# Layer 1's expert routing taken batch by batch into the attention to the context, in a decoder kernel on one core

## The chip, the cores and the metric

The kernel runs on one core of a Trainium2 chip. The metric is device time in microseconds (us). A core has five engines, each with a queue of its own that it works through in order: PE (matrix products; PEld is its loading of weights), DVE (vector), ACT (scalar functions), POOL and SP (which here issues DMAs). They wait for one another by semaphores.

## The reference

The program is one pass of a decoder over 8 batches of 256 tokens with 256 features. Four layers each do self-attention, attention to a context (120 rows for each batch) and a feed-forward part, each followed by a layer norm of the sum with its input. The change concerns layer 1, its attention to the context and its feed-forward part, which is a mixture of 32 experts:

```
logits = x @ gate_w.T                       # 2048 tokens x 32 experts
topk_w, topk_idx = top_k(softmax(logits), 4);  topk_w /= sum(topk_w)
# sorted by expert, then by token: pos = place of the token in its expert's list
slot = minimum(pos, 256)                    # 256 rows for each expert
buf[expert, slot] = x[token]
expert_out = (silu(buf @ w_gate) * (buf @ w_up)) @ w_down
routed[token] += expert_out[expert, slot] * topk_w      # where pos < 256
out = routed + (silu(x @ shared_gate) * (x @ shared_up)) @ shared_down
```

The place of a token in an expert's list is the number of earlier choices of the same expert, so the batches are bound together by running counts. The rows that an expert takes (the "take") are the lists turned round: for each expert and place the number of the token.

## The kernel before, in words

X lies in 16 tiles of 128 tokens, two for each batch; xT is its transpose. Code is written as functions for each part of a layer. A scheduler sets the order of instructions in each engine's queue within what dependencies, buffers and the order of the code allow; a tile pool has a fixed number of buffers for each tag, and a tile waits until the buffer that it takes over has been released.

**Attention to the context, layer 1** (`l1_xattn`, L792, which calls `attention16`, L703). A loop runs over the 8 batches. An iteration for batch b has: exponentials of b's scores (`exps16`; PE scores, ACT exp L627, buffers of the tag e0, two of 8 KB for each partition); the largest scores of batch b+1 (`largest16`, DVE reductions to `low`, L572; `lower16`, L609); the output projection, residual and layer norm of batch b-1 (`project_out`, L688: z L693, statistics L176 and L177, the reciprocal root on POOL L154 and L156, X L200); the keys and values of a later attention (`context3`, L833); the transposes of batch b-1 (`turn`, L696) and then its gate (`choose`, L818). Last come the sums of batch b (`sums16`, L665, and `divided16`, L645: transposes L651, reciprocals L654, `sides` on ACT L660 and DVE L661, aT on POOL L663). After an even batch the next two batches are projected (`pair`). After the loop `for step in before: step()` runs `project_out` and `turn` of batch 7.

`choose(b)` stores the two tiles of X to DRAM (L821, from which the experts gather), makes the logits (PE; ACT copies them as lg, L827) and takes the eight largest and their indices (DVE, L830 and L831).

Behind the loop stand eight sums of absolute weights of a later layer on ACT, `size` (L863), with buffers of the tag e0 too, and additions of partial sums on POOL (L865).

**Routing and experts** (`l1_ffn`, L1328). SP loads the shared expert's weights sgu and sd. POOL sums w_sums over partitions (an all-reduce, L1342). The shared expert's first product runs over 8 pieces of 256 tokens (8 fp32 matmuls, silu on ACT and a product on DVE, L1224 and L1225, into shT). `route1` (L1227) then routes all 16 tiles at once: `oh` says for token, choice and expert whether it was chosen (L1239); counts before each tile (L1254); places by products with a triangle and with ones (`pos`, L1261 and L1262) and DVE's at_own and place (L1266 to L1274); `own`, tile number and row number of each token at its expert (DVE L1258, ACT L1257). For every tile and choice `at` says which of 256 places the token has: 48 on DVE (L1282), 16 on ACT in two steps (off L1285, at L1286). 128 matmuls sum at times own into `found` (L1288), and `take` is made of it (L1295). Slots and weights are turned by 32 small matmuls (L1320) for a later stage.

The loop over 32 experts follows: its weights `we` (SP, three buffers), two gathers of 128 rows (POOL, L991, called from `gathered_T`), transposes, two products with silu between them, and the store of y. Every fourth expert also adds two tiles of the shared expert's second product. Work for a later layer is woven in.

Of the kernel before, what the change touches and what calls it, by code (L numbers as in the profile page):

```python
# [11 lines left out]
F32 = mybir.dt.float32  # L12
# [8 lines left out]
P = 128  # L21
# [25 lines left out]
class Net:  # L47
    def __init__(self, ctx: ExitStack, tc: tile.TileContext, ins, out):
# [52 lines left out]
        self.ahead = {}  # L101

# [600 lines left out]
    def attention16(self, project, low, vps, sizes, causal, wo, bo, work, then=None, ready=None):  # L703
# [45 lines left out]
        for step in before:  # L749
            step()  # L750
# [41 lines left out]
    def l1_xattn(self, w):  # L792
        nc = self.nc
        wq, wk, wv, wo, wk3, wv3, bv, bo = w
        with ExitStack() as ctx:
# [18 lines left out]
            zero = work.tile([1, D], F32, name="zero", bufs=1)  # L814
# [32 lines left out]

            def inside(b):
                return lambda: None, lambda: context3(b), lambda: None
# [3 lines left out]
                ready=(lambda: None, lambda: None, inside),  # L853
            )
# [372 lines left out]
    def route1(self, E, K, C, pool, work, ps, keep):  # L1227

        nc = self.nc
        fi = pool.tile([P, NT, K], F32, name="fi")
        nc.vector.tensor_copy(fi, self.top1_i[:, :, :K])
        iota = pool.tile([P, C], BF16, name="iota_bf")
        for o in range(0, C, 64):
            nc.vector.tensor_scalar(iota[:, o : o + 64], self.cst("iota"), float(o), None, ALU.add)
        oh = pool.tile([P, K, NT, E], BF16, name="oh")
        for k in range(K):
            nc.vector.tensor_tensor(  # L1239
                oh[:, k],  # L1240
                self.cst("iota")[:, :E].unsqueeze(1).to_broadcast([P, NT, E]),
                fi[:, :, k : k + 1].to_broadcast([P, NT, E]),
                ALU.is_equal,
            )
        m2 = pool.tile([P, 2, NT, E], BF16, name="m2")
        m = pool.tile([P, NT, E], BF16, name="m")
        before = pool.tile([P, NT + 1, E], BF16, name="before")
        nc.vector.memset(before[:, 0, :], 0.0)
        own = pool.tile([P, K, 2, NT, E], BF16, name="own")
        with nc.allow_low_precision(reason="whole numbers of at most 256"):  # L1250
            nc.vector.tensor_tensor(m2, oh[:, :2], oh[:, 2:], ALU.add)
            nc.vector.tensor_tensor(m, m2[:, 0], m2[:, 1], ALU.add)
            for i in range(NT):
                nc.vector.tensor_tensor(before[:, i + 1, :], before[:, i, :], m[:, i, :], ALU.add)  # L1254

        for i in range(NT):
            nc.scalar.mul(own[:, :, 1, i, :], oh[:, :, i, :], float(i))  # L1257
        nc.vector.tensor_scalar(own[:, :, 0], oh, self.cst("token")[:, 0:1], None, ALU.mult)  # L1258
        pos = ps.tile([P, NT, E], F32, name="pos")
        for i in range(NT):  # L1260
            nc.tensor.matmul(pos[:, i, :], lhsT=self.earlier, rhs=m[:, i, :], start=True, stop=False)  # L1261
            nc.tensor.matmul(pos[:, i, :], lhsT=self.ones_bf, rhs=before[:, i, :], start=False, stop=True)  # L1262
        pos_bf = pool.tile([P, NT, E], BF16, name="pos_bf")
        nc.scalar.copy(pos_bf, pos)
        at_own = pool.tile([P, K, NT, E], BF16, name="at_own")
        nc.vector.tensor_tensor(at_own, oh, pos_bf.unsqueeze(1).to_broadcast([P, K, NT, E]), ALU.mult)  # L1266
        part = at_own.rearrange("p k t e -> p (k t) e")
        for n in (E // 2, E // 4):
            half = pool.tile([P, K * NT, n], BF16, name=f"half{n}")
            with nc.allow_low_precision(reason="one of them is not zero"):  # L1270
                nc.vector.tensor_tensor(half, part[:, :, :n], part[:, :, n:], ALU.add)
            part = half
# [55 lines left out]
    def l1_ffn(self, w):  # L1328
# [3 lines left out]
        with (  # L1332
# [30 lines left out]
            with (  # L1363
# [31 lines left out]
                for _ in ready:  # L1395
                    pass
# [1152 lines left out]
```

## Time and profile before

Three runs took 2208.16, 2210.34 and 2219.71 us. One more execution was profiled.

| | |
|---|---|
| median of the three runs | 2210.34 us |
| the profiled execution | 2212.67 us |
| its span, first to last instruction | 2210.9 us |
| mean granted clock of PE | 0.929 |
| busy: PE, DVE, ACT, POOL | 1898.2, 1555.0, 903.1, 681.7 us |
| store of X of batch 0, and of batch 7 | at 722.27 and 848.65 us |
| last logits copied (lg ends) | at 852.43 us |
| first gather of an expert's rows | at 890.70 us |

Times in a timeline count from the start of the span. A line of a timeline has the start, the length, engine, line, operation, output and inputs with their shapes, a count where equal ones are put together, and in brackets how long the engine was idle before, with what ended the idle time. "issue" there means that the profile shows nothing that was waited for.

### The profile page before, as it was taken

What the parts mean: (1) busy time and instruction counts of PE and PEld (TensorE: products, weight loads), DVE (VectorE), ACT (ScalarE), POOL (GpSimd) and SP (SyncE); (2) the same over time, 40 slices, a digit from 0 to 9 for tenths busy, and PEclk for the clock granted to TensorE, in tenths of its full rate; (3) what the DMA queues carried; (4) which work ended last, traced back from release to release, by engine and by line L of the source; (5) the groups of instructions that cost most, each with busy time, mean ns of one, the idle gap of its engine ahead of it and who ended that gap; (6) DMA issues with size and microseconds to landing.
All of it is one profiled execution on the core that took longest, in us unless ns stands there. A gap on an engine that the chain in (4) does not pass through costs nothing. (4 is left out here: it accounts for less than half of the span.)

```text
span 2210.9 us, 37517 instructions
## 1 busy us (share of the span) xinstructions
PE 1898.2 (86%) x13553; PEld 1395.7 (63%) x13564; DVE 1555.0 (70%) x5150; ACT 903.1 (41%) x2002; POOL 681.7 (31%) x739
## 2 busy tenths in 40 slices
PE   7997699799999997897888876767899999998886
PEld 5765588655556665674455543456777777876775
DVE  6766443356666776773677678879999999976675
ACT  1333333233343336221334432534465545656663
POOL 1012244311111110544442100336544444430232
PEclk9999699999999997898899988888999999999998
DMA  4000354300002111684110010123322233320000
GB/s 139 2 2 11 117 179 148 121 26 2 1 1 86 43 43 65 179 241 140 46 40 22 1 72 1 55 77 110 87 80 76 68 89 87 86 89 14 6 15 21
DMA packets 71540, 148.55 MB, mean 67 GB/s; under 512 B 16984, under 2 KB 39912, under 8 KB 68272
## 3 DMA queue, kind: packets, MB, share of 16 engines
q0 software_dynamic: 32640, 79.46, 12.4%
q1 hardware_dynamic: 34074, 59.22, 8.2%
q10 hardware_dynamic: 4630, 7.36, 1.0%
q8 instruction: 111, 1.82, 0.3%
q14 instruction: 85, 0.70, 0.1%
HBM read 170.42 MB, written 23.24 MB: 88 GB/s over the span
## 5 line engine op out<-in xcount | busy, mean ns | idle before, releaser
L991 POOL DMA_INDIRECT rows<-in_l2f_table_dram,index x240 | 253.6, 1057 | 280.1 <-PE po L1784 59.8
L145 PE MATMUL pp<-xT,w 128*128 128x256 f32 (+1 forms) x672 | 175.3, 403 | 12.2 <-ACT sim L1490 4.6
L663 POOL TENSOR_TENSOR aT<-sides,inv 128x256 f32<-128x256 f32 x64 | 47.0, 737 | 367.8 <-DVE sides L661 271.9
L145 PEld LDWEIGHTS pp<-xT,w 128*128 128x128 f32 x672 | 127.1, 196 | 37.3 <-ACT sim L1490 5.7
L187 ACT COPY xT<-pt 128x512 f32<-128x512 f32 x88 | 51.3, 585 | 200.8 <-PE pt L186 200.6
L186 PE MATMUL pt<-ident,X 128*128 128x128 f32 x352 | 70.3, 314 | 67.0 <-DVE X L200 41.6
L1784 PE MATMUL po<-rows,diag 128*128 128x256 f32 x384 | 108.7, 403 | 12.5 <-ACT diag L1783 12.0
L627 ACT ACTIVATE e<-sc 128x512 f32<-128x512 f32 (+1 forms) x146 | 77.4, 602 | 102.2 <-PE sc L555 69.8
L991 POOL DMA_INDIRECT xe<-xd,take x83 | 83.7, 1008 | 110.9 <-DVE take L1295 36.7
L555 PE MATMUL sc<-kv,qv 32*128 32x128 f32 (+2 forms) x1520 | 109.8, 327 | 6.6 <-DVE sides L661 3.7
L555 PE MATMUL sc<-qv,kv 32*128 32x128 f32 (+2 forms) x1352 | 107.1, 352 | 2.4 <-DVE sides L661 1.4
L154 POOL TENSOR_SCALAR rs_v<-ln_mv 128x2 f32<-128x2 f32 (+1 forms) x67 | 18.8, 282 | 289.2 <-DVE ln_mv L177 238.5
L186 PEld LDWEIGHTS pt<-ident,X 128*128 128x128 f32 x352 | 45.4, 155 | 99.1 <-issue 42.7
L145 PE MATMUL sc<-xT,w 128*128 128x512 f32 x220 | 104.4, 624 | 2.9 <-DMA w<-in_l0a_wq_dram 2.2
L555 PEld LDWEIGHTS sc<-kv,qv 32*128 32x128 f32 x1520 | 86.5, 198 | 30.9 <-issue 18.6
L200 DVE TENSOR_SCALAR X<-z,ln_mv,rs_y 128x256 f32<-128x256 f32 x144 | 55.1, 425 | 59.4 <-POOL rs_y L156 59.3
L1149 ACT ACTIVATE hT<-ph,we_in 128x128 f32<-128x128 f32 x152 | 55.8, 367 | 96.6 <-PE ph L145 81.8
L1702 DVE SCALAR_TENSOR_TENSOR junk<-rows,X 128x256 f32<-128x256 f32 x224 | 94.2, 421 | 1.3 <-DVE dots L1773 0.2
L555 PEld LDWEIGHTS sc<-qv,kv 32*128 32x128 f32 (+1 forms) x1352 | 76.3, 196 | 26.5 <-issue 16.3
L145 PE MATMUL ph<-xeT,we_in 128*128 128x128 f32 x608 | 89.8, 292 | 1.3
L145 PEld LDWEIGHTS ph<-xeT,we_in 128*128 128x128 f32 x608 | 79.7, 198 | 12.3 <-ACT hT L1149 9.8
L1784 PEld LDWEIGHTS po<-rows,diag 128*128 128x128 f32 x384 | 68.0, 193 | 28.2 <-ACT diag L1783 16.7
(580 smaller groups left out, 5172.6 us busy)
## 6 DMA issues: line engine op xcount, KB each, us to landing
we<-in_l1f_experts_dram SPq DMA_DIRECT2D x32, 384.0 KB, 4.2
yd<-y SPq DMA_DIRECT2D x32, 256.0 KB, 3.9
w<-in_l2x_w_dram SPq DMA_DIRECT2D x1, 4096.0 KB
v<-v SPq DMA_DIRECT2D x16, 243.8 KB, 2.9
rows<-in_l2f_table_dram,index POOLq DMA_INDIRECT x240, 3.4
xd<-X SPq DMA_DIRECT2D x8, 257.0 KB, 2.8
xT<-in_xT_dram SPq DMA_DIRECT2D x4, 512.0 KB, 7.7
X<-in_x_dram ACTq DMA_DIRECT2D x8, 256.0 KB, 6.1
```

The lines of the kernel that those rows point to most:

```text
L145: self.nc.tensor.matmul(out, lhsT=lhsT, rhs=rhs, start=n == 0, stop=n == last and bias is None)
L154: nc.gpsimd.tensor_scalar(v, var, LN_EPS, None, ALU.add)
L186: nc.tensor.transpose(pt[:, c, j, :], self.X[:, i0 + j * step, c * P : (c + 1) * P], self.ident)
L187: nc.scalar.copy(self.xT4[:, :, i0 : i0 + step + 1 : step, :], pt)
L200: nc.vector.tensor_scalar(self.X[:, i, :], z[:, j, :], mv[:, j, 0:1], r[:, j : j + 1], ALU.subtract, ALU.mult)
L555: nc.tensor.matmul(sc[: shape[0], part], lhsT=lhsT, rhs=rhs, start=mask is None, stop=True, skip_group_check=True)
L627: lambda r, sc: nc.scalar.activation(e0[m][:n0, r], sc, AF.Exp),
L663: nc.gpsimd.tensor_tensor(out, split(both), split(inv), ALU.mult)
L991: return self.nc.gpsimd.indirect_dma_start(out=out, out_offset=None, in_=table, in_offset=bass.IndirectOffsetOnAxis(ap=index, axis=0), **( ...
L1149: nc.scalar.activation(hT[:, g + f, :], ph[:, f, :], AF.Gelu, bias=b1[:, g + f : g + f + 1])
L1702: nc.vector.scalar_tensor_tensor(junk, row, 1.0, x, ALU.mult, ALU.mult, accum_out=out)
L1784: nc.tensor.matmul(po, lhsT=diag, rhs=rows[:, k, D:], start=j == 0 and (g, k) == (0, 0), stop=j == 1 and (g, k) == (groups[-1][0], here_k ...
```

## The change

`route1` is taken apart. `begin_route1` allocates before the attention. `places1(b)` makes one-hot, counts, pos and places of one batch, `takers1(b)` its own, at and found, summed over batches into `found1`; `shared1(b)` is the shared expert's first product of one batch. The loop's iteration b runs `places1(b-2)` first and, for b of 2 to 5, `takers1(b-2)` last. After the loop, ahead of `project_out` of batch 7: places of 6, takers of 4 and 5, shared 0, 1, 2; ahead of its `turn`: takers of 6, shared 3 and 4; behind it: places and takers of 7, `end_route1` (the take, and logits less the largest), shared 5, 6, 7. The silu of `shared1` takes buffers of the tag e0. sgu and shT come from a pool that is open from ahead of the attention to the end of `l1_ffn`, and the row of zeros is the first of shT. `at_own` and pos are fp32, `off` has one buffer, `oh` four. Slots are turned after expert 2 (`slots1`), weights after the last expert (`weights1`), each with 16 of the 32 small matmuls. The `size` sums and the all-reduce are where they were in the code. The core of the diff:

```diff
@@ -746,7 +747,9 @@
-        for step in before:
+        for fill, step in zip(tail, (*before, lambda: None)):
+            if fill:
+                fill()
             step()
 
     def project16(self, dst, w, src, bias, n, kind):
@@ -811,7 +814,7 @@
                     self.values16(vp[:, n, 0, :], pv, SC, bv)
                 return qv, kv
-            zero = work.tile([1, D], F32, name="zero", bufs=1)
+            zero = self.shT[0:1, :D]
             nc.gpsimd.memset(zero, 0.0)
             nc.sync.dma_start(self.xd1[0:1, :], zero)
@@ -845,12 +848,40 @@
                 nc.vector.tensor_copy(v[:, :, :64], pv[:SC].rearrange("p (h d) -> p h d", d=64))
                 nc.sync.dma_start(self.v3[b], v.rearrange("p h d -> p (h d)"))
+            INLOOP = 4
+
             def inside(b):
-                return lambda: None, lambda: context3(b), lambda: None
+                def early():
+                    if b >= 2:
+                        self.places1(b - 2, work)
+
+                def last():
+                    if 2 <= b < 2 + INLOOP:
+                        self.takers1(b - 2, work)
+
+                return early, lambda: context3(b), last
+
+            def fill(places, takers, shared):
+                def steps():
+                    if places is not None:
+                        self.places1(places, work)
+                    for n in range(max(len(takers), len(shared))):
+                        for b in takers[n : n + 1]:
+                            self.takers1(b, work)
+                        for b in shared[n : n + 1]:
+                            self.shared1(b, work)
+
+                return steps
+
+            def finish():
+                fill(B - 1, [B - 1], [])()
+                self.end_route1(work)
+                fill(None, [], [5, 6, 7])()
             self.attention16(
                 project, low, vps, [SC], False, wo, bo, work, then=choose,
                 ready=(lambda: None, lambda: None, inside),
+                tail=(fill(B - 2, list(range(INLOOP, B - 2)), [0, 1, 2]), fill(None, [B - 2], [3, 4]), finish),
             )
             o = 0
@@ -1224,138 +1255,160 @@
-    def route1(self, E, K, C, pool, work, ps, keep):
...
+    def places1(self, b, work):
+        tiles = slice(2 * b, 2 * b + 2)
+        fi = self.fi1[:, tiles]
+        nc.vector.tensor_copy(fi, self.top1_i[:, tiles, :K])
+        oh = self.oh1[b % 4]
+        nc.vector.tensor_tensor(
+            oh,
+            self.cst("iota")[:, :E].unsqueeze(1).unsqueeze(1).to_broadcast([P, K, 2, E]),
+            fi.rearrange("p t k -> p k t").unsqueeze(3).to_broadcast([P, K, 2, E]),
+            ALU.is_equal,
+        )
+        here, following = self.counts1[b % 2], self.counts1[1 - b % 2]
+        with nc.allow_low_precision(reason="whole numbers of at most 256"):
+            nc.vector.tensor_reduce(here[:, 1:], oh.rearrange("p k t e -> p t e k"), AX.X, ALU.add)
+            if b + 1 < B:
+                nc.vector.tensor_reduce(following[:, 0, :], here.rearrange("p t e -> p e t"), AX.X, ALU.add)
+        pos = self.bank([P, 512])[:, : 2 * E].rearrange("p (t e) -> p t e", t=2)
+        for out, lhsT, rhs in (
+            (pos, self.earlier, here[:, 1:]),
+            (pos[:, 0], self.ones_bf, here[:, 0]),
+            (pos[:, 1], self.ones_bf, here[:, 0]),
+            (pos[:, 1], self.ones_bf, here[:, 1]),
+        ):
+            nc.tensor.matmul(out, lhsT=lhsT, rhs=rhs, start=lhsT is self.earlier, stop=True, skip_group_check=True)
+        at_own = work.tile([P, K, 2, E], F32, name="at_own", bufs=1)
+        nc.vector.tensor_tensor(at_own, oh, pos.unsqueeze(1).to_broadcast([P, K, 2, E]), ALU.mult)
+        nc.vector.tensor_reduce(self.place1[:, :, tiles], at_own, AX.X, ALU.add)
+    def takers1(self, b, work):
+        oh = self.oh1[b % 4]
+        own = work.tile([P, K, 2, 2, E], BF16, name="own", bufs=1)
+        nc.vector.tensor_scalar(own[:, :, 0], oh, self.cst("token")[:, 0:1], None, ALU.mult)
+        for j in range(2):
+            nc.scalar.mul(own[:, :, 1, j, :], oh[:, :, j, :], float(2 * b + j))
+        found = self.bank([P, 512])[:, : 4 * E].rearrange("p (b a e) -> p b a e", b=2, a=2)
+        for j in range(2):
+            for k in range(K):
+                at = work.tile([P, C], BF16, name="at", bufs=4)
+                where = self.place1[:, k, 2 * b + j : 2 * b + j + 1]
+                if k < K - 1:
+                    nc.vector.tensor_scalar(at, self.iota1, where, None, ALU.is_equal)
+                else:
+                    off = work.tile([P, C], BF16, name="off", bufs=1)
+                    nc.scalar.activation(off, self.iota1, AF.Abs, bias=where, scale=-1.0)
+                    nc.scalar.activation(at, off, AF.Relu, scale=-1.0, bias=self.one)
+                for half in range(2):
+                    nc.tensor.matmul(
+                        found[:, half], lhsT=at[:, half * P : (half + 1) * P], rhs=own[:, k, :, j, :],
+                        start=j == 0 and k == 0 and half == 0, stop=j == 1 and k == K - 1, skip_group_check=True,
+                    )
+        if b:
+            nc.vector.tensor_tensor(self.found1, found, self.found1, ALU.add)
+        else:
+            nc.vector.tensor_copy(self.found1, found)
+    def shared1(self, b, work):
+        ph = self.bank([P, 2, 256])
+        for m in range(2):
+            self.mm(
+                ph[:, m, :],
+                [(self.sgu[:, c, m * P : (m + 1) * P], self.xT[:, c, b * S : (b + 1) * S]) for c in range(2)],
+            )
+        g = work.tile([P, S], F32, name="silu", tag="e0")
+        nc.scalar.activation(g, ph[:, 0, :], AF.Silu)
+        nc.vector.tensor_tensor(self.shT[:, b * S : (b + 1) * S], g, ph[:, 1, :], ALU.mult)
+    def end_route1(self, work):
+        nc.vector.scalar_tensor_tensor(
+            self.take1.rearrange("p n b -> p b n"), self.found1[:, :, 1, :], float(P), self.found1[:, :, 0, :],
+            ALU.mult, ALU.add,
+        )
+        best, K = self.top1, self.K1
+        nc.vector.tensor_tensor(
+            self.best1, best[:, :, :K], best[:, :, 0:1].to_broadcast([P, NT, K]), ALU.subtract
+        )
...
     def l1_ffn(self, w):
...
+            take = self.take1.rearrange("p n b -> p (n b)")
...
+                    if e == 2:
+                        self.slots1(self.route1, ps2.tile([P, 512], F32, name="pp"))
...
                 for _ in ready:
                     pass
+                self.weights1(self.route1, ps2.tile([P, 512], F32, name="pp"))
@@ -2521,7 +2577,16 @@
             net.power = name in POWER
+            if name == "l1_xattn":
+                route = ctx.enter_context(ExitStack())
+                pool = route.enter_context(tc.tile_pool(name="f1k", bufs=1))
+                net.sgu = pool.tile([P, 2, 256], F32, name="sgu")
+                net.nc.sync.dma_start(net.sgu, ins["l1f_sgu"].rearrange("p (c n) -> p c n", c=2))
+                net.shT = pool.tile([P, NTOK], F32, name="shT")
+                net.begin_route1(pool)
             getattr(net, name)(w)
+            if name == "l1_ffn":
+                route.close()
             w = net.ahead[following] if following in INSIDE else nxt
         if "l2_ffn" in layers:
```

## The prediction

> **What bounds the kernel now.** I read the page's engine totals first: PE is busy 86% of the span and DVE 70%, so no engine is the bound throughout and the stage decides. Layer 1's context attention and its expert stage lie at 675 to 1021 us. I cut that stretch into windows at the stores of X that `choose` issues (L821, one for each batch), at the end of the routing and at the start of the expert loop. Columns: window, length, busy us of PE, PEld, DVE, ACT, POOL, then the granted clock, DMA share and GB/s.
>
> ```profile
> 739.97:761.68 21.71, 21.49 (x200) 15.20 (x199) 16.69 (x47) 8.98 (x17) 3.64 (x5) 1.00 0.11 36
> 761.68:777.77 16.09, 14.83 (x173) 10.54 (x172) 13.09 (x35) 6.42 (x13) 3.47 (x5) 1.00 0.15 49
> 832.80:852.50 19.70, 12.31 (x68) 7.69 (x66) 6.92 (x25) 11.27 (x23) 2.60 (x5) 0.69 0.16 53
> 852.50:890.40 37.90, 27.55 (x256) 21.83 (x256) 27.66 (x116) 25.37 (x63) 0.49 (x1) 0.77 0.20 67
> 890.40:1010.00 119.60, 110.77 (x545) 90.67 (x550) 81.11 (x156) 30.37 (x64) 64.95 (x64) 0.95 0.76 223
> ```
>
> In the attention loop (first two rows) PE is nearly full in an iteration that also projects a pair, and DVE has 3.0 us free in one without. The tail after the last sums (third row) is loose on every engine and PE's clock falls to 0.69. The routing (fourth row) is 38 us in which no engine is full and POOL waits for the gather's indices. The waits say it, in us, times, longest; then POOL's timeline (start, length, idle before it), and DVE's for one loop iteration and for the tail:
>
> ```profile
> POOL xe L991 <- DVE take L1295: 36.7, 1, 36.7
> POOL w_scale L1342 <- issue: 5.7, 1, 5.7
> ```
>
> ```profile
> 853.52 0.49 POOL L1342 PARTITION_ALL_REDUCE w_scale<-w  x1 [5.66 <-issue]
> 890.70 1.19 POOL L991 DMA_INDIRECT xe<-xd,take  x1 [36.69 <-DVE take L1295]
> ```
>
> ```profile
> 767.22 0.29 DVE L830 MAX8 w<-lg 128x8 f32<-128x32 f32 x2 [1.26 <-ACT lg L827]
> ...
> 774.14 0.69 DVE L693 TENSOR_TENSOR z<-pt,biased 128x512 f32<-128x512 f32 x1 [0.22 <-PE pt L145]
> ...
> 777.01 0.73 DVE L200 TENSOR_SCALAR X<-z,ln_mv,rs_y 128x256 f32<-128x256 f32 x2 [1.17 <-POOL rs_y L156]
> ```
>
> ```profile
> 845.06 0.69 DVE L693 TENSOR_TENSOR z<-sc,biased 128x512 f32<-128x512 f32 x1 [3.84 <-PE sc L145]
> ...
> 852.46 0.29 DVE L830 MAX8 w<-lg 128x8 f32<-128x32 f32 x2 [3.83 <-ACT lg L827]
> ```
>
> Those three gaps, 2.65 us, are all that DVE waits for in the iteration, and each ends on work that DVE had just fed: the loop without a projection is a nearly closed DVE chain.
>
> **Removed.** From the last logits (lg ends at 852.43) to the first gather (890.70) pass 38.3 us. All of it goes, and what the new kernel puts between these two points is priced below: **-38.3**.
>
> **Added in the loop.** Each batch's `places1` and `takers1` bring to DVE, by rows of the routing and half sizes of them: fi 0.15 (a 128x1 operation takes 0.147 at L2110), oh 0.37 (a 128x512 one takes 0.686), two counts 0.38 (a 512-wide reduce takes 0.681) and 0.17, at_own 0.42 (the 128x256 multiply at L1225), place 0.40, own 0.16, six `at` of 0.23 each (three run in 0.68), found 0.26: 3.7 us. The built queue order puts places and takers of batches 0 to 3, places and three `at` of batch 4 and places of batch 5 into the loop: 4 x 3.7 + 2.7 + 1.9 = 19.4. PE gets 16 `found` of 0.076 and four `pos`, 1.5; ACT own, off and at, 2.3, of which it has 9 us free. Places stand behind the maximum of the same batch and ahead of the second `sides`, of the next `low` and of z. In an iteration without a projection I let 3.1 of 3.7 count, since only the part that stands directly ahead of a wait is taken up. With a projection PE's queue is the bound (21.49 of 21.71), DVE's gaps are larger, and 2.0 counts, PE's 1.5 and a little. By store intervals: 2.6 + 2.0 + 3.1 + 2.0 + 3.1 + 1.2 = **+14**. Bounds: 7 (PE's 1.5 in four, 0.5 in two) and 19.4.
>
> **Added in the tail.** Between the last sums (838.2) and the last output projection PE gets shared products 0, 1, 2 (8 matmuls, 2.0 each at full clock), `found` 4 and 5 (0.6 each) and pos: 7.4 into a gap of 2.96, so +4.4; the warmer PE then does w,aT in 2.0, not in 3.90: z +2.5. DVE's takers 5 and the found add stand between z and X: X +4.3. X's transposes are queued behind `found` 6, whose `at` follow X on DVE, and shared 4, at 855.8 where they were at 848.45. The gate's matmuls take 1.1, not 1.92. lg comes **+6.5** later; 3 if found 6 doesn't wait for X, 9 if three products run at the slow price (5.88 for two at 856.21).
>
> **After the last logits.** Count from lg's end. DVE's maxima, oh and counts 1.5, pos, at_own and place to 2.7, three `at`, `found` 7 and the take at 6.8. But the take no longer comes last. ACT's order is a table load, Exp, own, off, at, off, at, a table load, silu of shared 5, 6, 7, and then the eight `size` sums of L863. Those use buffers of tag e0, which the silus now take too. Before, they ran in ACT's idle time ahead of lg:
>
> ```profile
> 837.42 0.63 ACT L863 ACTIVATE size<-w 128x512 f32<-128x512 f32 x1 [0.43 <-PE pt L676]
> ...
> 844.71 1.90 ACT L863 ACTIVATE size<-w 128x2048 f32<-128x2048 f32 x1
> ...
> 852.22 0.21 ACT L827 COPY lg<-sc 128x64 f32<-128x64 f32 x1 [2.01 <-PE sc L145]
> ```
>
> Shared 7 leaves PE at 8.9, silus end at 9.3. `size` takes 9.28 (837.42 to 846.70), 8.5 without two `sides` in it, so it ends at 17.8. On POOL the add of the second long sum (15.9) stands ahead of the all-reduce, the all-reduce waits for all sums, and the gathers are queued behind it. What took 5.66 of "issue" ahead of the all-reduce then begins at 16: 21.7, plus 0.49 and 0.3: first gather at **+22.5**. Bounds: 18.6 if those 5.66 lie beside `size`; 25 if the silus are 2.5 late. Behind the same wait are queued on SP sd, the first expert weights and layer 2's weights, and on DVE the context work at 890.81.
>
> Three table loads now stand in the tail, and none carries this sum, since ACT waits for `place` and for PE between them. What one costs, the routing shows:
>
> ```profile
> 864.12 1.28 ACT L1311 ACT_TABLE_LOAD   x1
> 865.41 0.26 ACT L1311 ACTIVATE picks<-picks 128x64 f32<-128x64 f32 x1
> 865.68 1.28 ACT L1224 ACT_TABLE_LOAD   x1
> ```
>
> Exp starts where the load ends, with no gap, and so does the next load. The Trainium skill (page "ScalarE: Activation LUTs", section "What ACT_TABLE_LOAD costs") charges a drain of 1.38 us on top of the 1.283 us load at every switch of sets. By it three switches would be 8.0 us, not 3.9, and the gather up to 2 us later; the row speaks against it.
>
> **Start and end of the experts.** Loads of 2 MB (expert weights, sd, layer 2's) ran at 854 to 870 beside the routing; now they meet the first gathers in a stage whose DMA share is 0.76: +1 (0, since the first expert's weights may land during its gather, which lands in 4.3 in this stage; 4, about one landing of 4.2). `weights1`'s 16 transposing matmuls stand in the PE-bound loop (110.77 of 119.60): +1 (0 to 1.1, the 32 at L1320 took 1.1 busy).
>
> **Sum.** -38.3 + 22.5 + 14 + 6.5 + 1 + 1 = **+6.7**. On the profiled execution (2212.67, span 2210.9) that is 2219.4; it lies 2.3 above the median 2210.34, so against the median: **2217**. About 0.5%, 11 us, is what a measurement of this kernel can tell from no change. All low ends give -38.3 + 18.6 + 7 + 3 = -9.7, all high ends -38.3 + 25 + 19.4 + 9 + 4 + 1.1 = +20.2.
>
> **Rivals.** (1) *DVE pays in full, slower.* If the loop's DVE chain is closed in every iteration, all 19.4 count: +12.1, 2222; it ends over 0.5% from a loop cost of 18.4 on. Where ACT's `off`, which waits for `place`, also holds up the next exps by 1 us in four iterations: 2226. For: 13.09 busy of 16.09 and all gaps fed by DVE itself. Against: gaps of 2 to 3 us in projecting iterations.
> (2) *The gaps hide it.* Six gaps of 2.65 leave 3.5 of the 19.4, and the tail costs 3: -7.3, 2203. For: DVE is only 70% busy and PE's weight loads fill 10.54 of 16.09. Against: the gaps move with DVE's work.
> (3) *`size` doesn't gate the gather*: it goes at the take, 7.3: +6.7 - 15.2 = -8.5, 2202; with (2) 2188. For: it ran in the shade before. Against: the built queues of ACT and POOL as above.
> (4) *The change doesn't do what it says*, routing work staying behind the last logits: the scheduler putting it back there; the time would stay at 2210. The queue order excludes it for batches 0 to 6.
>
> **Chances.** Forecast 0.47, (1) 0.27, (2) 0.18, (3) 0.08. Faster by over 0.5% (under 2199.3) takes (3) with (2), or one of them with a cheap start: 0.15. Slower (over 2221.4) takes (1) and the upper part of the forecast: 0.33. Between: 0.52. Range 2201 to 2230, from all low ends to all high ends.
>
> **What would show it.** In the changed kernel's profile: store intervals 2 to 3 us longer each (under 1: rival 2; 3.7: rival 1); ACT's `size` behind the last silu; POOL's gap ahead of the first gather ended by `size` or issue, not by the take (else rival 3); lg to gather 20 to 25 us; expert weights landing later than 4.2 us. A PE clock under 0.9 in the loop or a store interval that shrinks would make all this wrong.

## The result, and the profile after

The changed kernel is slower: 2226.63 us median of 9 runs, against 2209.76 for before, ratio 1.0073 (95% interval 1.0055 to 1.0092), so 16 us with 12 to 20 as bounds. Its profiled execution took 2223.78, with a span of 2222.0 and a mean granted clock of 0.925. The prediction said 2217 and gave "slower by over 0.5%" a chance of 0.33.

The windows of the changed kernel, cut at the same events, show where the time came from. Columns as before.

```profile
723.56:742.67 19.11, 17.59 (x177) 12.30 (x176) 15.74 (x45) 8.24 (x18) 3.47 (x5) 0.91 0.13 41
742.67:767.78 25.11, 23.13 (x220) 15.88 (x219) 20.17 (x61) 11.30 (x23) 3.66 (x5) 1.00 0.10 31
767.78:788.27 20.49, 19.43 (x193) 13.65 (x192) 16.42 (x49) 8.76 (x19) 3.45 (x5) 0.92 0.12 39
788.27:813.38 25.11, 23.15 (x220) 15.91 (x219) 20.06 (x61) 11.30 (x23) 3.67 (x5) 1.00 0.10 32
813.38:835.43 22.05, 20.99 (x193) 14.54 (x192) 16.22 (x49) 8.76 (x19) 3.46 (x5) 0.85 0.11 35
835.43:852.68 17.25, 15.58 (x117) 9.50 (x116) 12.39 (x36) 6.86 (x14) 2.40 (x4) 0.90 0.14 45
852.68:879.16 26.48, 22.14 (x159) 15.76 (x157) 14.81 (x55) 10.59 (x26) 2.53 (x4) 0.94 0.12 39
```

Every iteration but the last (17.25, before 17.09) is clearly longer than before, and in the two without a projection PE's clock is below full (0.92 and 0.85, where it was 1.00). Behind the last logits (they end at 879.16) the shape is the one forecast. ACT's timeline, then POOL's, of the changed kernel:

```profile
889.31 0.38 ACT L1346 ACTIVATE silu<-sc 128x256 f32<-128x256 f32 x1 [1.03 <-PE sc L146]
889.59 0.62 ACT L894 ACTIVATE size<-w 128x512 f32<-128x512 f32 x1
...
896.01 1.89 ACT L894 ACTIVATE size<-w 128x2048 f32<-128x2048 f32 x1
```

```profile
896.18 0.19 POOL L896 TENSOR_TENSOR w<-w,more 128x1 f32<-128x1 f32 x1 [25.50 <-ACT size L894]
901.97 0.49 POOL L1410 PARTITION_ALL_REDUCE w_scale<-w  x1 [5.60 <-DMA we<-in_l1f_experts_dram]
902.65 1.35 POOL L1022 DMA_INDIRECT xe<-xd,take  x1 [0.19 <-issue]
```

The take was ready at 887.19, 8.0 us after the logits. The gather waited 15.5 us more: the last silu, the eight `size` sums, the addition, the start of the all-reduce, the all-reduce. The profile puts the 5.60 us ahead of the all-reduce down to a load of expert weights, which the all-reduce does not use; before showed 5.66 with "issue", and I read both as its start. POOL's gap of 36.7 us named by the take is now one of 25.5 named by `size`.

The change between the two profiled executions, section by section:

| section | before | changed | difference | forecast |
|---|---|---|---|---|
| span's start to the first store of X | 722.27 | 723.56 | +1.3 | 0 |
| first to seventh store (loop) | 110.53 | 129.12 | +18.6 | +14 |
| seventh store to the last logits (tail) | 19.63 | 26.48 | +6.9 | +6.5 |
| last logits to the first gather | 38.27 | 23.49 | -14.8 | -15.8 |
| first gather to layer 2's first gather | 133.34 | 130.86 | -2.5 | +2 |
| the rest of the span | 1186.86 | 1188.49 | +1.6 | 0 |
| sum | 2210.9 | 2222.0 | +11.1 | +6.7 |

### The profile page after: what moved, and what is told of

It reads as the page before. It is cut to its first block, busy times and chain, and to the rows that moved or that the text cites. A ratio compares the mean times of both kernels' runs of the same rounds, so it can differ in the third digit from the quotient of the medians.

```text
span 2222.0 us, 37602 instructions
## 1 busy us (share of the span) xinstructions
PE 1914.2 (86%) x13596; PEld 1403.3 (63%) x13596; DVE 1561.9 (70%) x5185; ACT 903.6 (41%) x1999; POOL 680.0 (31%) x739
## 5 line engine op out<-in xcount | busy, mean ns | idle before, releaser
L187 PE MATMUL pt<-ident,X 128*128 128x128 f32 x352 | 71.0, 318 | 63.5 <-DVE X L201 38.3
L146 PE MATMUL sc<-xT,w 128*128 128x512 f32 x204 | 96.6, 623 | 3.1 <-DMA w<-in_l0a_wq_dram 2.4
L146 PEld LDWEIGHTS ph<-xeT,we_in 128*128 128x128 f32 x608 | 80.5, 200 | 12.3 <-ACT hT L1180 9.8
```

Source lines behind the costliest of these rows:

```text
L146: self.nc.tensor.matmul(out, lhsT=lhsT, rhs=rhs, start=n == 0, stop=n == last and bias is None)
L187: nc.tensor.transpose(pt[:, c, j, :], self.X[:, i0 + j * step, c * P : (c + 1) * P], self.ident)
```

## The experiments

Numbers that come back in all of them: "loop" is from the first to the seventh store (before 110.5), "tail" from the seventh store to the end of the last logits (before 19.6), "gather" from there to the first gather (before 38.3), "experts" from there to the first gather of layer 2's attention (before 133.3). Theory: the loop and the tail pay for DVE's added instructions as worked out, and the gather waits for the `size` sums that the silus had pushed behind them. Runs 7 to 9 fell on a chip on which before took 2266.9, the others on chips on which it took 2208 to 2211; ratios are always to before on the same chip, the sections to before's one profile.

| run | loop | tail | gather | experts | ratio (95% interval) |
|---|---|---|---|---|---|
| changed | 129.1 | 26.5 | 23.5 | 130.9 | 1.0073 (1.0055 to 1.0092) |
| changed, again | 129.4 | 28.6 | 24.3 | 132.8 | 1.0099 (1.0068 to 1.0130) |
| 1 silus off e0 | 128.7 | 32.6 | 12.3 | 133.7 | 1.0068 (1.0042 to 1.0094) |
| 2 no routing in the loop | 111.2 | 42.5 | 24.7 | 135.4 | 1.0060 (1.0040 to 1.0080) |
| 4 all-reduce behind gathers | 127.4 | 25.8 | 19.6 | 139.4 | 1.0116 (1.0086 to 1.0146) |
| 5 silus off e0, all-reduce behind y | 128.6 | 31.7 | 11.2 | 137.2 | 1.0055 (1.0031 to 1.0079) |
| 6 as 5, size in the loop | 128.7 | 29.3 | 12.4 | 137.0 | 1.0057 (1.0030 to 1.0084) |
| 7 as 6, matmul with ones | 129.1 | 26.5 | 11.6 | 136.0 | 1.0042 (1.0015 to 1.0069) |
| 8 as 7, places only in the loop | 119.7 | 37.7 | 11.3 | 135.6 | 1.0038 (1.0019 to 1.0058) |
| 9 as 7, routing from iteration 7 on | 110.6 | 35.7 | 13.0 | 135.1 | 0.9983 (0.9964 to 1.0002) |
| 10 as 9, spread further | 110.4 | 26.0 | 19.3 | 134.2 | 0.9981 (0.9969 to 0.9994) |
| 11 changed, every at on DVE | 128.1 | 25.2 | 23.9 | 133.3 | 1.0046 (1.0025 to 1.0067) |

**What holds the gather** (runs 1, 4, 5, 6, 7). The smallest edit is run 1:

```diff
-        g = work.tile([P, S], F32, name="silu", tag="e0")
+        g = work.tile([P, S], F32, name="silu", tag="k3")
```

> The changed kernel with one word changed: shared1's silu takes a buffer of the tag k3, not e0. Theory (e0 alone put the size sums behind the silus): the sums run right behind the last attention sums, the gather comes 8 to 12 us after the last logits where it was 23.5. But POOL's queue now has the all-reduce, and with it its start, ahead of the layer norm of batch 7, so the last X can come up to 11 us later; time 2 to 10 us under the changed kernel on the same chip, the upper part if that start lies in POOL's idle time. Rival (something else holds the gather): 18 us or more after the logits.

The gather came 12.3 us after the logits, 11 us earlier, so the tag alone had put the sums there. It does not go at the take even so: here the take was ready at 893.56 and the gather started at 896.80, and in runs 1 and 5 to 9 the profile ends POOL's wait with the last product into shT. The price named in the expectation came too: the tail is 4 to 6 us longer than in the two executions of the changed kernel. On this chip the time is 7 us under the changed kernel's 2229.5, by six executions each, but the two intervals in the table overlap, and the first measurement of the changed kernel gave 1.0073 against the 1.0068 here; a gain in time is not shown. POOL's timeline in this run, and two lines of ACT's and DVE's, show why.

```profile
865.06 0.19 POOL L896 TENSOR_TENSOR w<-w,more 128x1 f32<-128x1 f32 x1 [2.68 <-ACT size L894]
871.32 0.49 POOL L1410 PARTITION_ALL_REDUCE w_scale<-w  x1 [6.08 <-ACT size L894]
878.68 0.24 POOL L155 TENSOR_SCALAR rs_v<-ln_mv 128x2 f32<-128x2 f32 x1 [6.87 <-DVE found L1332]
```

```profile
870.89 0.20 ACT L894 ACTIVATION_READ_ACCUMULATOR size<-w 128x1 f32 x1
```

```profile
872.67 0.18 DVE L178 BATCH_NORM_AGGREGATE ln_mv<-ln_st 128x2 f32<-128x6 f32 x1
```

The last sum ended at 871.09, 0.23 us ahead of the all-reduce, so this row does not tell a start from a wait for ACT. The next ordinary operation is the layer norm of the last batch. It reads ln_mv, which DVE had ready at 872.85, and starts 5.8 us later; in the changed kernel the same operation starts 0.1 us after ln_mv. The bracket names `found`, but that ended 0.8 us ahead. Other executions agree. In before, the changed kernel and run 6 only gathers follow the all-reduce on POOL until `biased` in layer 2's attention, and POOL is idle for 7.2, 7.2 and 7.4 us ahead of that; in run 1, where the layer norm came first, and in runs 7 and 10, which have no all-reduce, it is not idle there. So going back to ordinary operations costs some 6 to 7 us once, and run 1 pays it ahead of the last X.

Run 4 leaves the sums late and moves only the all-reduce:

```diff
-            nc.gpsimd.partition_all_reduce(self.w_scale, self.w_sums[:, : len(L2X)], P, bass_isa.ReduceOp.add)
...
+                    if e == 1:
+                        nc.gpsimd.partition_all_reduce(
+                            self.w_scale, self.w_sums[:, : len(L2X)], P, bass_isa.ReduceOp.add
+                        )
```

> The all-reduce stands behind the gathers of the first two experts on POOL; nothing else is moved. Theory (its 5.6 us of start and 0.5 stand between the size sums and the first gather): the gather comes at the end of the size sums, 18.5 to 19.5 us after the last logits where it was 23.5, and the time falls by 3 to 5 us, to 2222 to 2224. Rival (the 6 us only move behind the first gathers and hold up those of expert 2 as much): gather earlier, time within 1 us of the changed kernel. Second rival (something else than POOL's queue holds the gather): gather still at 22 or later.

The gather came at 19.6, about as the theory said. The time did not fall: the 6.07 us of start now stand between the gathers of experts 1 and 2 (POOL: 897.13 to 904.14), the eighth store of y comes 44.8 us after the first gather where it came 38.2 in the changed kernel, and the section of the experts is 8.5 us longer. The first rival was right, and more than right.

Run 5 takes the silus off e0 and makes the all-reduce wait for expert 0's y. It computes the same sums, plus 0 times y.

```diff
+                    if e == 0:
+                        sums = self.w_sums[:, : len(L2X)]
+                        nc.vector.scalar_tensor_tensor(sums, y[:, 0, : len(L2X)], 0.0, sums, ALU.mult, ALU.add)
+                        nc.gpsimd.partition_all_reduce(self.w_scale, sums, P, bass_isa.ReduceOp.add)
```

> shared1's silu takes a buffer of the tag k3 instead of e0, and the all-reduce waits for expert 0's y (the sums get 0 times y added). Theory (the size sums gate the gather because the silus took their buffers): the size sums run right behind the last attention sums, the gather comes 8 to 11 us after the last logits; ACT's 8.5 us of sums now stand ahead of the last takers' at, which can hold z up by up to 4. Time 9 to 14 us under the changed kernel: 2213 to 2218. Rival (the gather is held by what else is late there, the expert weights or the release of the attention's memory): gather 18 us or more after the logits, time 2222 to 2227.

The gather was as expected (11.2). The time, 2223.3, was not: of the 12 us won there, 5 went to the tail (ACT's sums now stand ahead of `at`) and 6 to the experts. Run 6 takes the sums out of the tail:

```diff
+                    if b < 4:
+                        next(size, None)
+                        next(size, None)
...
+                        nc.scalar.activation(
+                            self.shT[:, :m], self.l2x_flat[:, o + a : o + a + m], AF.Abs, accum_out=total
+                        )
```

> As the run before, but the size sums run in the loop's iterations 0 to 3, their output thrown into shT, which is free there, so that no ACT work is added to the tail. Theory: ACT has 9 to 12 us free in an iteration, so the loop is within 1.5 us of the changed kernel's, the tail is not longer, the gather comes 8 to 11 us after the last logits: 12 to 16 us under the changed kernel, 2211 to 2215, so no faster than before within 0.2%. Rival (in order on ACT the sums hold up the next exponentials): the loop is 4 to 8 us longer and the time 2217 to 2222.

The loop was not longer (128.7), so the rival fell: ACT has room there. The gather (12.4) and the tail (+2.8) were each a little later than expected, the experts again took 137.0, and so the time was 2221.3 and not 2211 to 2215. Run 7 replaces the all-reduce by one matmul:

```diff
+                nc.vector.memset(every, 1.0)
+                whole = ps2.tile([P, 512], F32, name="pp")
+                nc.tensor.matmul(
+                    whole[:, : len(L2X)], lhsT=every, rhs=self.w_sums[:, : len(L2X)], start=True, stop=True
+                )
+                nc.scalar.copy(self.w_scale, whole[:, : len(L2X)])
```

> As the run with the size sums in the loop, but the sum over partitions is one matmul with ones on PE ahead of the experts instead of the all-reduce on POOL. Theory (the all-reduce's start on POOL, 6.9 us with 0.5 of work, stood between the gathers of experts 5 and 6 there and cost 4 to 6 us): from the first gather of the experts to the first gather of layer 2's attention it takes 131 to 133 us again, where it was 137.0; the time is 4 to 6 us under that run, 2215 to 2218. Rival (those 7 us lay beside PE's work): 136 or more, time 2220 to 2223.

136.0 and not 131 to 133: the number is the rival's. It does not clear the all-reduce of runs 5 and 6, because something else moved too. In run 6 the fourth y is stored 7.3 us behind the third, and the all-reduce stands between them; in run 7 it is 2.8. But the third comes 25.0 us after the first gather in run 7 and 21.5 in run 6. SP's timeline of run 7 shows a candidate for that; the first gather of that run starts at 887.44.

```profile
887.64 0.38 SPq L1437 DMA_DIRECT2D we<-in_l1f_experts_dram  x1
888.16 0.54 SPq L125 DMA_DIRECT2D w<-in_rows_dram  x2
888.74 0.35 SPq L133 DMA_DIRECT2D w<-in_l2a_wq_dram  x1
...
891.32 12.68 SPq L1437 DMA_DIRECT2D we<-in_l1f_experts_dram  x3
```

The first weights start 0.2 us after the first gather, where they ran 36.5 us ahead of it in before and 4.1 ahead in the changed kernel, and layer 2's weights are queued between the first expert's and the second's. The first y is stored 17.0 us after the first gather, where it was 14.6 and 14.2. So a late gather may give part of its lateness back, which would be the -2.5 of the changed kernel. No run moved these loads alone, and run 2 does not fit: there the weights start 4.3 us ahead of the gather, as in the changed kernel, and yet the first y comes 16.8 us after it and the section takes 135.4. What sets the experts' section stays open.

**What the loop pays for** (runs 2, 8, 11, 9). Run 2 takes the routing out of the loop:

```diff
+                return lambda: None, lambda: context3(b), lambda: None
+
+            def behind():
+                for b in range(B - 1):
+                    fill(b, [b], [])()
+                fill(None, [], [0, 1, 2])()
```

> Routing of batches 0 to 6 moves out of the loop to behind the last sums, one batch after the other, ahead of the shared products 0 to 2. Theory (the loop pays for DVE's added instructions, 13 to 14 us, and for the drops of PE's clock that come with them, 4 to 5 us): the store intervals go back to those of before (17.7, 21.7, 16.1, 21.1, 16.8, 17.1, each within 0.7) with the clock of before, so 18 us are saved ahead of the seventh store; behind the last sums DVE has some 19 us more, of which 8 to 11 fall into its idle time, so the last logits come 7 to 11 us earlier than in the changed kernel and the time is 2216 to 2220. Rival (the loop is slower for another reason, the turn of the PSUM banks or the new pool): the intervals stay 10 us or more longer in sum and the time is 2235 to 2245.

The loop went back to 111.2, single intervals within 1.1 of before's, so the routing, with the clock drops that come with it, is the whole cause there. The second half of the expectation failed: 16 of the 18 us came back in the tail, not 8 to 11, because z, X and the gate stood behind all of it in DVE's and PE's queues; so the time was 2224.3 and not 2216 to 2220.

Run 8 leaves only `places1` in the loop, on top of run 7:

```diff
-            INLOOP = 4
+            INLOOP = 0
...
-        self.oh1 = [pool.tile([P, K, 2, E], BF16, name=f"oh{n}") for n in range(4)]
+        self.oh1 = [pool.tile([P, K, 2, E], BF16, name=f"oh{n}") for n in range(8)]
...
-            z = work.tile([P, 2, D], F32, name="z")
+            z = work.tile([P, 2, D], F32, name="z", bufs=1)
```

> As the run with the ones matmul, but the loop holds only places1; takers1 of batches 0 to 6 run behind the last sums (oh in eight buffers, z in one). Theory (each part is paid for by DVE's time): of the 3.7 us of a batch 1.8 are takers, so from the first to the seventh store it takes 119 to 123 us, where the changed kernel took 129.1 and before 110.5; from there to the last logits 5 to 10 us more than the 26.5 of the changed kernel, so the time is within 3 us of the run with the ones matmul. Rival (the loop pays for the chain from counts through PE's pos to the places, which stands in DVE's and PE's queues, not for the takers): 125 us or more in the loop and a slower kernel by 3 to 8 us.

119.7, inside the expectation: places cost 9 us and takers 9 in the loop, clock drops included. The tail is 11 us longer (expected 5 to 10), and the time the same as run 7's. What z in one buffer costs by itself was not separated. By iteration, from the windows of run 8 (the third interval, without a projection, and the fourth, with one, both at full clock):

```profile
772.64:790.14 17.50, 16.11 (x177) 11.83 (x176) 14.54 (x41) 6.33 (x13) 3.44 (x5) 1.00 0.14 46
790.14:812.08 21.94, 21.73 (x204) 15.58 (x203) 18.37 (x53) 8.78 (x17) 3.65 (x5) 1.00 0.11 35
```

from run 6, where both parts are in the loop and the clock stayed full in the fifth interval, without a projection, and from before, the fifth too:

```profile
811.68:830.88 19.20, 18.14 (x193) 12.53 (x192) 16.38 (x49) 8.76 (x19) 3.45 (x5) 1.00 0.12 40
```

```profile
798.87:815.71 16.84, 14.51 (x173) 10.68 (x172) 13.10 (x35) 6.32 (x13) 3.45 (x5) 1.00 0.14 46
```

Without a projection the third interval is 16.09 (before) and 17.50 with places: 1.4, as much as DVE's busy time rose (13.09 to 14.54). The fifth is 16.84 (before) and 19.20 with both parts: 2.4, where DVE's busy time rose by 3.3. The third with both parts never ran at full clock, so the takers' own part is only bounded, by 1.0 (2.4 less 1.4) and 1.7 (19.20 less 17.50). With a projection it is 21.10, 21.94 and 25.11: 0.8 for places, but 3.2 for takers. The waits of the changed kernel in 788.27 to 813.38 name it, ACT's first and then PE's:

```profile
ACT off L1324 <- DVE place L1304: 2.4, 1, 2.4
```

```profile
PE sc L146 <- ACT e L628: 1.0, 1, 1.0
```

In a projecting iteration the scheduler puts `at_own` and `place` behind the projections' DVE work, ACT's `off` waits 2.4 us for `place`, and the next exponentials are queued behind `off`; PE then waits 1.0 for them. Run 11 takes `off` out of ACT's queue, against more DVE work:

```diff
-                if k < K - 1:
+                if k < K:
                     nc.vector.tensor_scalar(at, self.iota1, where, None, ALU.is_equal)
```

> The changed kernel, with the fourth choice's at made on DVE like the other three, so that ACT has no off in its queue: 0.5 us more of DVE in each batch, 1.8 to 2.0 less of ACT. Theory (in a projecting iteration the places come late, ACT's off waits 2.4 us for them, and the next exponentials behind it hold up PE by 1.0): the projecting iterations get shorter in spite of DVE's work, from 25.1 to between 23.6 and 24.6; the others, where the places come early, get 0.2 to 0.6 longer at the same clock. Rival (the projecting iterations pay for PE's found products and for DVE): 25.4 to 25.8. The time moves by less than 5 us either way.

```profile
745.67:770.09 24.42, 23.47 (x220) 16.20 (x219) 20.41 (x63) 9.49 (x19) 3.65 (x5) 1.00 0.10 32
```

25.11 became 24.42 although DVE has two instructions more (63, not 61); PE's wait for the exponentials is gone from that iteration, and the others got 0.1 to 0.3 longer at the same clock. So the mechanism is shown, for 0.7 to 1 us an iteration. The rest of those 3.2, some 2.4, goes with the takers (PE's found products and DVE's at); which of the two was not separated.

**The clock** (the changed kernel again):

> The changed kernel once more, for a second profile. Theory (the loop's longer iterations come in fixed sizes, and PE's clock drops add to them from one execution to the next): the store intervals without a drop are the same as in the first profile within 0.2 us (25.1 with a projection); those with a drop (20.5 and 22.0 in the first) lie between 19.2, the value of the experiments at full clock, and 22.1; gather 23 to 24 us after the last logits; slower than before by 12 to 20 us. Rival (the clock drops belong to fixed places of the code): intervals and clocks as in the first profile within 0.2 us.

```profile
743.85:768.96 25.11, 23.13 (x220) 15.89 (x219) 20.16 (x61) 11.29 (x23) 3.66 (x5) 1.00 0.10 31
768.96:789.45 20.49, 19.43 (x193) 13.58 (x192) 16.49 (x49) 8.75 (x19) 3.46 (x5) 0.92 0.12 39
789.45:815.99 26.54, 24.58 (x220) 16.23 (x219) 20.06 (x61) 11.29 (x23) 3.67 (x5) 0.94 0.09 30
815.99:836.50 20.51, 19.45 (x193) 13.43 (x192) 16.49 (x49) 8.74 (x19) 3.44 (x5) 0.92 0.12 38
```

The same program, on another execution: 25.11 is 26.54 where the clock was 0.94, and 22.05 at 0.85 is 20.51 at 0.92. At full clock the intervals repeat to 0.1 us. The drops of the fourth and fifth intervals come and go and add 1.3 to 2.9 each; for these the rival, fixed places, fell. The third interval's does not: it is 20.49 at 0.92 in both executions, 20.49 to 20.61 at 0.92 in runs 1, 4, 5, 6 and 11, and 21.95 at 0.84 in run 7. With the whole routing in the loop it never ran at full clock. This execution's span was 2230.3, 19.4 over before's profile, with the same sections (the loop +18.9, the gather -14.0).

**A version that beats both** (runs 9 and 10). Only DVE's idle time is free, so the routing goes where it is: two batches into iteration 7, which has no next batch's scores, the rest into the tail. Run 9, on top of run 7:

```diff
-                    if b >= 2:
-                        self.places1(b - 2, work)
+                    if b == B - 1:
+                        self.places1(0, work)
...
-                    if 2 <= b < 2 + INLOOP:
-                        self.takers1(b - 2, work)
+                    if b == B - 1:
+                        self.takers1(0, work)
+                        fill(1, [1], [])()
...
+            def first():
+                for b in (2, 3):
+                    fill(b, [b], [b - 2])()
+
+            def second():
+                for b in (4, 5):
+                    fill(b, [b], [b - 2])()
```

> As the run with the ones matmul, but iterations 0 to 6 hold no routing: batches 0 and 1 are routed in iteration 7, 2 and 3 ahead of the last output projection, 4 and 5 ahead of the last transposes, 6 and 7 behind them, with the shared products 0 to 3 between. Theory (only DVE's idle time is free: 6.6 us in the last iteration and 12 in the tail of before, and none in the loop): the first five store intervals are those of before within 0.7 us, the last one 1 to 4 us longer, the last logits come 38 to 44 us after the seventh store, the gather 9 to 12 after them; 4 to 10 us faster than before, 2200 to 2206. Rival (z and X stand behind the routing in DVE's queue, so its idle time isn't used): logits 46 us or more after the seventh store, time 2212 to 2220.

Run 9 has the first five intervals within 0.6 of before (18.3, 21.7, 16.6, 21.1, 16.8), the last 1 us shorter and not longer (at a clock of 1.00, where before had 0.90), the logits 35.7 and the gather 48.7 after the seventh store. It is 3.8 us faster than before by the ratio, with no change just inside the interval: less than the 4 to 10 expected. Run 10 puts as little as possible ahead of z and X:

```diff
+            def first():
+                fill(2, [2], [])()
+
+            def second():
+                fill(3, [3], [0, 1])()
+
+            def finish():
+                fill(4, [4], [2, 3])()
+                fill(5, [5], [4, 5])()
+                fill(6, [6], [6, 7])()
+                fill(B - 1, [B - 1], [])()
+                self.end_route1(work)
```

> As the run that routes from iteration 7 on, but only batch 2 stands ahead of the last output projection and batch 3 with shared 0 and 1 ahead of the last transposes; batches 4 to 7 with shared 2 to 7 follow. Theory (in DVE's and PE's queues z and X stood behind routing there): z 5 to 7 us earlier, the last logits 27 to 31 us after the seventh store where they were 35.7, the take 14 to 18 us after them, the gather 44 to 47 us after the seventh store where it was 48.7. So 2 to 4 us faster than that run and 5 to 9 us faster than before. Rival (DVE's time is full there, so order doesn't matter): gather 48 us or more after the seventh store and 3 to 5 us faster than before, as that run.

Logits after 26.0, gather after 45.2 (expected 44 to 47), 2203.68 against 2208.03, 1 to 7 us faster than before. This is the one version clear of before, and by less than the 5 to 9 us expected; the profile's own section from the first store to layer 2's gather is 12.0 us shorter (289.8 against 301.8). That flatters it: the profiled execution of run 10 was its fastest, 2197.53, 6 us under its median, and before's, 2212.67, lies 5 us above the median on this chip. The windows of run 10 show the loop as it was, and a shorter last iteration:

```profile
775.66:796.75 21.09, 20.89 (x200) 15.01 (x199) 16.86 (x49) 9.09 (x17) 3.65 (x5) 1.00 0.12 37
796.75:813.59 16.84, 14.51 (x173) 10.68 (x172) 13.20 (x36) 6.32 (x13) 3.47 (x5) 1.00 0.15 46
813.59:829.73 16.14, 13.63 (x117) 8.69 (x116) 12.92 (x39) 8.21 (x17) 2.40 (x4) 1.00 0.15 48
```

The last iteration of before:

```profile
815.71:832.80 17.09, 14.67 (x112) 9.32 (x111) 10.47 (x30) 6.34 (x14) 2.39 (x4) 0.90 0.15 46
```

In the last iteration of run 10 DVE holds 12.92 us of work, 2.45 more than in before's, in less time; the clock is 1.00 there and was 0.90 in before, which PE's busy time (13.63 against 14.67) shows too.

## Why the prediction was right, and where its sum was off

The time fell into the stated range, near its upper end, and the waits behind the last logits were those forecast. The loop was not, and part of the agreement is luck: in the first profile the loop's error of +4.6 and the experts' of -4.5 cancel. Of the signs named, `size` behind the last silu, POOL's gap, 20 to 25 us to the gather and later expert weights (4.8 us to land, not 4.2) came. "Store intervals 2 to 3 us longer each" did not: they are longer by 1.4, 3.4, 4.4, 4.0, 5.2 and 0.2, so three of them pass the 3.7 that was to show rival 1. And "a PE clock under 0.9 in the loop", which was to make all this wrong, came, with 0.85 in the fifth interval. Step by step:

- **The gather waits for size and the all-reduce.** Forecast 22.5 after the logits, measured 23.5 and 24.3; the silus end at 10.5 (forecast 9.3), `size` at 18.8 (17.8), the start took 5.60. Rival 3 fell, and its price was too low as well: without `size` ahead of it the gather came 11.2 to 13.0 after the logits and not 7.3, behind the last shared product. Run 1 shows that the buffers' tag alone put `size` there. The row, not the rule, was right on the table loads: in the changed kernel the load at 886.33 takes 1.28 and the silu follows at 887.62.
- **The tail.** Forecast 6.5, measured 6.9 and 9.0.
- **The start of the experts.** Forecast +2, measured -2.5 and -0.5. Mis-sized in the other direction, for a reason that stays open: that a gather which comes 12 us later finds part of its first wait already served is a reading, which run 2 does not bear out. Runs 1 and 5 to 7, with early gathers, show the forecast's sign (+0.4 to +3.9).
- **The loop.** Forecast 14, measured 18.6 and 18.9. This is the term that was mis-sized, in two places. "With a projection PE's queue is the bound, DVE's gaps are larger, and 2.0 counts" failed: it was 3.4 and 4.0, of which 0.7 to 1 is ACT's `off` ahead of the exponentials, named in rival 1 but priced only there. And the clock: I took the loop's 1.00 as given. The two iterations without a projection lost 1.3 and 2.9 us to it, if the 19.20 at full clock of run 6's fifth interval holds for both. Without these 4.1 the loop is +14.5, near the forecast, but by errors that cancel: the first and last intervals cost less than I said (1.4 and 0.2, not 2.6 and 1.2). DVE's own added time was over-priced too: its busy time in the loop rose by 17.9 us (83.1 to 101.0) and not by 19.4.
- **Rival 1** (DVE pays in full) gave 2222 to 2226 and is nearest to the measured time, but not for its reason alone: the one iteration without a projection that ran at full clock paid 2.4 of the 3.3 by which DVE's busy time rose (the forecast let 3.1 of 3.7 count).

What is left open is the size of the total. Two profiles give +11.1 and +19.4, the timed runs +16 and +22. The +11.1 and the +16 differ mostly by the choice of execution: before's profiled one lay 2.9 us above its median and the changed kernel's 2.9 below. The mean granted clock over the span was 0.924 and 0.925 in the timed executions of the changed kernel and 0.930 in those of before, and within before and the changed kernel 0.001 of clock goes with 1.1 to 1.8 us, so 5 to 10 us of the difference go with the clock. The loop's drops do not explain that. They lose 8.4 us of clock time (length times the missing share) where before lost 3.5, but the tail and the wait for the gather, at 0.94 and 0.71 where they were at 0.69 and 0.77, lose 8.4 where before lost 14.9. The lower mean lies behind layer 2's first gather, with 0.92 in the changed kernel and 0.93 in before; run 10 has 0.92 there too, so nothing ties it to the change.

## What to carry to other kernels

Work moved into a loop is free only where the engine that does it waits for something that is not fed by itself; a gap in the waits that moves with the engine's own work is not room, and the queue of a second engine (here ACT's `off` ahead of the exponentials) can add to the price (0.7 to 1 us an iteration here). When a buffer tag is lent to a new user, list who else takes that tag and what waits for them. A saving that ends at a shared gate, here the all-reduce ahead of the gathers, is worth only the distance to that gate; look first at what can come last after it.

## What was not expected of the hardware

PE's clock halved after short losses of PE work. In the changed kernel, windows of 2 us show it (PE, PEld, DVE, ACT, POOL busy, clock):

```profile
821.56:823.56 2.00, 1.32 (x12) 0.81 (x10) 2.00 (x6) 1.31 (x4) 0.74 (x1) 1.00 0.00 0
823.56:825.56 2.00, 2.00 (x10) 1.22 (x12) 1.53 (x7) 0.65 (x2) 0.71 (x1) 0.60 0.00 0
825.56:827.56 2.00, 2.00 (x22) 1.71 (x24) 1.30 (x6) 0.34 (x1) 0.03 (x1) 0.50 0.00 0
827.56:829.56 2.00, 2.00 (x27) 1.70 (x21) 0.65 (x2) 1.97 (x5) 0.00 (x0) 0.50 0.03 8
829.56:831.56 2.00, 2.00 (x8) 1.48 (x6) 1.71 (x4) 0.68 (x2) 0.00 (x0) 0.69 0.00 0
831.56:833.56 2.00, 2.00 (x45) 1.78 (x44) 1.66 (x5) 0.71 (x2) 0.98 (x1) 1.00 0.00 0
```

The only idle time of PE here is 0.68 us in front of 823.41, and the eight matmuls of the output projection took 2.95 us at 828.81 where they took 1.97 at 807.57. Such a gap alone does not decide: in before PE is idle for 0.67 us in front of 803.09, in an iteration whose clock stays at 1.00. The Trainium skill (page "TensorE: Matmul & The Clock Gate", section "Part 1: The HAM clock gate (the "warmup" mystery)") says that the clock falls to half after an idle window of about 3.4 us, and that the window runs freely, so that the same kernel can meet it differently. The second fits the two profiles of one program, with drops at different places; the first does not, since PE was idle for 0.68 us and not for 3.4.

POOL's all-reduce has a start of 5.66 us in before and 6.07 in run 4, both named "issue"; the gathers right behind it start after 0.19. Going back to an ordinary operation took 5.8 us in run 1, and POOL was idle for 7.2 us ahead of the first one in before. The Trainium skill (page "GPSIMD Engine Reference", section "2.1 Instruction dispatch") gives about 6 us for the first call of freshly loaded code. The start agrees with it in size; that code is loaded there no run shows. A matmul with ones did the same sum in 0.36 us of PE (run 7).
